# Two layers of attention on one core: which accesses to a PSUM ring are declared independent of each other

## The chip, the cores and the metric

The kernel runs on one core of a Trainium2 chip, in one launch. Its time is the device time of one execution in microseconds (us), and the kernel before is given by the median of three runs. The profile comes from one further execution that was recorded by the hardware profiler.

The engines named here: TensorE (PE in the profile; PEld are its weight loads), VectorE (DVE), ScalarE (ACT), GpSimd (POOL) and SyncE (SP). SP and POOL issue DMAs, each in the order of its own queue.

## The reference

Two images of 256 channels and 64 x 64 pixels pass through two layers; each adds to its input a function of the group-normalised input. Cut to layer 0, which the change concerns:

```python
x = x + _L0_conv_ref(_gn(x), qkv_w, qkv_b, 8)

qkv = jnp.einsum('bchw,oc->bohw', x, qkv_w) + qkv_b[None, :, None, None]
qkv = qkv.reshape(b, 3, num_heads, head_dim, n)          # 8 heads of 32, n = 4096
attn_logits = jnp.einsum('bhci,bhcj->bhij', q, k) * scale
attn_weights = jax.nn.softmax(attn_logits, axis=-1)
out = jnp.einsum('bhij,bhcj->bhci', attn_weights, v)
```

So each head of each image has 4096 x 4096 scores; each row is exponentiated, divided by its sum and multiplied with the values. Group normalisation (32 groups of 8 channels) needs a mean and a variance for each group. Layer 1 is another attention in blocks of 8 x 8 pixels beside a 3 x 3 convolution; the change does not touch it.

## The kernel before

The kernel is written with a framework that finds the dependences between instructions by the tiles they access and inserts semaphore waits. Within layer 0's attention the order on TensorE, ScalarE and VectorE is the order in which the program emits instructions (`manual_schedule`, line 795); SP's and POOL's queues are ordered by the framework.

**Units and groups.** For each image (`b`, two of them) `attention0` runs over 16 groups: 8 heads by 2 halves of the queries. A group has 32 blocks `j` of 128 keys, and each block has 4 units `u` of 512 queries. A unit is a score product of 128 keys by 512 queries (line 522, TensorE), which fills one bank of PSUM, and the exponential of that bank (line 531, ScalarE), which writes a slot in SBUF. There are 28 slots; the profile calls them `es` or `v`, after the two tiles that hold them.

**The ring.** One PSUM tile, `ring`, has 7 banks, used in turn. `scores()` emits one round of 9 units in phases of 1, 1, 3, 2 and 2 (`PHASE`): so many score products, then one exponential over all their banks. A phase is split where it would pass the end of the ring or of the slots. The framework takes a tile as a whole; so in `scores()` each score product is declared independent of the recent exponentials of other banks, and each exponential independent of the recent score products into other banks (`tc.declare_no_dep`).

**What follows the scores.** With a lag of at least 7 units, `work_of` adds a block's exponentials to running sums on VectorE (`add_rows`, lines 572 and 580, into `added`, named `e` in the profile) and multiplies them with the values on TensorE (`quarters`, line 543, four products of 32 columns each, into the accumulator `av`). Seven blocks of a group (`SUMMED`) are not added by VectorE but by accumulating DMAs on POOL's queue (lines 588 and 590), whose result VectorE adds in at the start of the next group (line 770). A slot may be written again when VectorE or the DMA, and TensorE, have read it.

**Spare banks.** Now and then another product needs a bank. `spare_bank()` takes the next bank of the ring out of its turn. Three kinds of use go through the list `wanted`; the main loop takes the bank after a round of scores and runs the use after two further steps of work:

- the sums of rows of the group before (`finish` and `sum_rows`): eight products of `ones` with `added` through `quarters` (line 543, `ring<-e,ones`), then a ScalarE copy out of the bank (line 620, `avs<-ring`). This happens 15 times per image;
- the mean for layer 1's normalisation (`means`, line 318, and the copy of line 319), once per image in the last group;
- the variance (`variances`, line 328, and the copy of line 726), once per image in the last group.

The last group's own sums of rows also use a spare bank, but they are emitted at the end of its scores, with other operands.

**After the sums.** The copied sums go out and back through memory on SP's queue: `dsum` (line 621), `dense` (line 623), the reciprocals on VectorE (lines 626 to 628, at block 9), `drec` (line 629), and back into `avs` (line 631). VectorE multiplies the group's result by them at block 17 (line 635). The same queue brings the next head's keys in four pieces of 512 KB (line 380), its values (line 384), the queries, and in later groups `o` (line 690).

## Time and profile before

| | us |
|---|---|
| median of 3 runs | 3133.02 (3130.93 to 3133.04) |
| the profiled execution | 3135.6 |
| its span, first to last instruction | 3133.7 |
| TensorE busy in the span | 3000.3 (96%) |
| VectorE busy | 2459.8 (78%) |
| ScalarE busy | 2343.5 (75%) |
| the exponentials of line 531 (2596 instructions) | 1985.6 busy |
| the score products of line 522 (4096) | 1081.9 busy |
| the sums of rows over whole banks, line 543 `ring<-e,ones` (240) | 32.8 busy, 49.3 idle before them |

Layer 0's attention of the first image lies from 120 to about 1170 us (with the second half of its projections at the start), of the second image from about 1660 to 2727 us. Between and after them lie layer 1 and the second image's projections, which the change leaves alone. One group of attention takes some 64 us: the sums of rows begin at 199.96, 263.85, 327.48, 391.23 us, and so on.

How to read it: TensorE's matmuls are pipelined, so a matmul's length is longer than the distance to the next one, and "busy" is not "at its peak". A number in brackets behind an instruction is the time its engine sat idle before it, with what ended that time. A wait costs time only where nothing else of equal length runs beside it.

### The profile page before, as it was taken

The page shows a single profiled execution, that of the slowest core. Times are in us where ns is not written, and L with a number is a line of the kernel's source. Part 1 is how long each engine was busy: PE and PEld are TensorE (multiplying, and loading weights), DVE is VectorE, ACT ScalarE, POOL GpSimd, SP SyncE. Part 2 cuts the span into 40 slices and gives each one's busy share as a digit, 9 for nine tenths or more (in the row PEclk, how much of TensorE's full clock was granted, in tenths as well). Part 3 has the DMA queues.
Part 4 walks back from the last instruction along what each step waited for, and adds up shares of the span by engine and source line. Part 5 has one row for each costly group of instructions (what it writes and reads, how often), then busy time and mean ns, then how long its engine had stood idle before and what let it go on. Part 6 is the DMA issues. An engine that isn't in the chain of part 4 may idle for free. (4 is left out here: it accounts for less than half of the span.)

```text
span 3133.7 us, 63967 instructions
## 1 busy us (share of the span) xinstructions
PE 3000.3 (96%) x25129; PEld 1864.8 (60%) x25129; DVE 2459.8 (78%) x3122; ACT 2343.5 (75%) x3262; POOL 836.2 (27%) x923
## 2 busy tenths in 40 slices
PE   6999999999999999999989999999999999899998
PEld 3555555555555556667755555555555555466765
DVE  4599989999899988856556998989988899834543
ACT  2699999999999974632237999999999999734333
POOL 2022222222222221055401222222222222305440
PEclk9999999999999999999999999999999999999999
DMA  7979679786897651231159787796878975600000
GB/s 237 272 136 179 142 152 178 144 176 150 163 180 161 138 126 35 64 125 49 41 186 266 134 169 152 155 181 138 173 161 163 182 152 126 166 4 4 21 14 22
DMA packets 243796, 424.48 MB, mean 135 GB/s; under 512 B 99112, under 2 KB 109916, under 8 KB 241308
## 3 DMA queue, kind: packets, MB, share of 16 engines
q0 software_dynamic: 94992, 238.36, 39.7%
q1 hardware_dynamic: 147580, 181.68, 21.3%
q8 instruction: 199, 3.26, 0.4%
q14 instruction: 113, 0.93, 0.1%
q10 hardware_dynamic: 912, 0.27, 0.0%
HBM read 119.03 MB, written 68.39 MB: 60 GB/s over the span
## 5 line engine op out<-in xcount | busy, mean ns | idle before, releaser
L531 ACT ACTIVATE es<-ring 128x512 f32<-128x512 f32 (+2 forms) x1572 | 1204.3, 905 | 34.8 <-PE ring L522 28.1
L580 DVE TENSOR_TENSOR e<-e,es 128x1024 f32<-128x1024 f32 (+1 forms) x956 | 1039.4, 1145 | 80.8 <-ACT es L531 80.1
L522 PE MATMUL ring<-q,k 128*128 128x512 f32 x4096 | 1081.9, 407 | 4.1 <-ACT es L531 1.9
L522 PEld LDWEIGHTS ring<-q,k 128*128 128x128 f32 x4096 | 733.5, 188 | 373.9 <-ACT es L531 115.6
L531 ACT ACTIVATE v<-ring 128x512 f32<-128x512 f32 (+2 forms) x1024 | 781.3, 902 | 33.7 <-PE ring L522 29.6
L543 PE MATMUL av<-es,v 128*32 128x256 f32 (+1 forms) x9684 | 726.6, 390 | 0.0
L580 DVE TENSOR_TENSOR e<-e,v 128x1024 f32<-128x1024 f32 (+1 forms) x636 | 671.0, 1109 | 49.8 <-ACT v L531 48.3
L543 PE MATMUL av<-v 128*32 128x256 f32 (+1 forms) x6188 | 496.9, 388 | 0.0
L543 PEld LDWEIGHTS av<-es,v 128*32 128x32 f32 x9684 | 328.2, 110 | 267.3 <-issue 108.4
L543 PEld LDWEIGHTS av<-v 128*32 128x32 f32 x6188 | 220.7, 109 | 170.8 <-issue 72.4
L590 POOL DMA_DIRECT2D es<-es x118 | 100.8, 854 | 508.9 <-ACT es L531 463.9
L975 PE MATMUL mm<-v,wf 128*128 128x256 f32 x1024 | 227.6, 380 | 1.5 <-DVE z L984 1.5
L975 PEld LDWEIGHTS mm<-v,wf 128*128 128x128 f32 x1024 | 193.3, 190 | 36.8 <-issue 9.8
L965 POOL TENSOR_TENSOR v<-col 128x512 f32<-128x512 f32 x128 | 165.2, 1316 | 180.1 <-DVE x L996 35.0
L980 ACT COPY z<-mm 128x512 f32<-128x512 f32 x32 | 18.7, 584 | 184.3 <-PE mm L975 184.3
L590 POOL DMA_DIRECT2D acc<-es x118 | 116.5, 987 | 114.2 <-ACT es L531 56.3
L588 POOL DMA_DIRECT2D es<-es x20 | 11.4, 568 | 504.7 <-ACT es L531 401.6
L590 POOL DMA_DIRECT2D es<-v x72 | 61.3, 852 | 316.7 <-ACT v L531 306.1
L981 DVE TENSOR_TENSOR z<-z,mm 128x512 f32<-128x512 f32 x32 | 22.0, 686 | 141.4 <-ACT z L980 141.0
L590 POOL DMA_DIRECT2D v<-es x112 | 114.9, 1026 | 24.3 <-ACT es L531 11.6
L590 POOL DMA_DIRECT2D acc<-v x78 | 77.1, 988 | 69.3 <-DMA acc<-es 23.9
L961 POOL TENSOR_TENSOR col<-xp 128x1152 f32<-128x1152 f32 x32 | 69.3, 2165 | 64.3 <-DVE xp L1394 53.0
(252 smaller groups left out, 2685.3 us busy)
## 6 DMA issues: line engine op xcount, KB each, us to landing
acc<-es POOLq DMA_DIRECT2D x128, 512.0 KB, 6.4
acc<-v POOLq DMA_DIRECT2D x84, 512.0 KB, 6.3
es<-es POOLq DMA_DIRECT2D x138, 256.0 KB, 4.1
v<-es POOLq DMA_DIRECT2D x132, 256.0 KB, 4.9
k<-wk_halves SPq DMA_DIRECT2D x64, 512.0 KB
q<-wq_halves SPq DMA_DIRECT2D x256, 128.0 KB
v<-v POOLq DMA_DIRECT2D x90, 256.0 KB, 5.1
es<-v POOLq DMA_DIRECT2D x84, 256.0 KB, 3.9
```

The costliest lines, as they stand in the source:

```text
L522: made = nc.tensor.matmul(sc[:, i, :], held["k", g // 2][:, j * P : (j + 1) * P], held["q", g, u // 2][:, u % 2, :], start=True, stop=True,)
L531: made = nc.scalar.activation(dst, sc, AF.Exp, scale=SC0)
L543: nc.tensor.matmul(dst[HD0 * u : HD0 * u + HD0, n], lhs, rhs(u)[:, n], start=start, stop=stop)
L580: nc.vector.tensor_add(dst[:, s, :], dst[:, s, :], src)
L588: nc.gpsimd.dma_start(out=dst, in_=src)
L590: nc.gpsimd.dma_start(out=dst, in_=src, accum_op=ALU.add)
L961: (nc.gpsimd.tensor_add if plus else nc.gpsimd.tensor_sub)(col, cols(one), cols(two))
L965: (nc.gpsimd.tensor_add if plus else nc.gpsimd.tensor_sub)(dst, rows(one), rows(two))
L975: nc.tensor.matmul(mm[:, m, r, :], wf[:, k, 4 * r + q, m * P : (m + 1) * P], v[r // 2][:, r % 2, k, :], start=k == 0, stop=k == KC - 1,)
L980: nc.scalar.copy(z[:, 1], mm[:, :, 1, :])
L981: nc.vector.tensor_add(z[:, 0], z[:, 1], mm[:, :, 0, :])
```

## The change

The bookkeeping that declares accesses independent is pulled out of `scores()` into a function `touch`, with one list for all engines, and the users of a spare bank are passed through it too: the first-to-fifteenth groups' sums of rows and their copy, the mean's and the variance's products, and their copies. An access is declared independent of every recent access by another engine to other banks. The list keeps the last 60 accesses, where the two lists before kept 21 each. The last group's own sums of rows are not passed through it. Line numbers shift: the score product moves from 522 to 535, the exponential from 531 to 541, `quarters` from 543 to 550, the copy of the sums from 620 to 627.

```diff
         def means(self, ks, pm, copy):
-            nc.tensor.matmul(pm, group8, self.mv[:, ks, 0], start=True, stop=True)
-            copy(self.mean[:, ks], pm)
+            return nc.tensor.matmul(pm, group8, self.mv[:, ks, 0], start=True, stop=True), copy(self.mean[:, ks], pm)
...
-        recent = {"pe": [], "act": []}
+        recent, spare = [], [0]
         ring = psum["sc"].tile([P, BANKS, T], F32, tag="ring", name=f"ring_{b}")
+
+        def touch(made, banks):
+            for engine, past, other in recent:
+                if engine != made.ins.engine and not banks & other:
+                    tc.declare_no_dep(made.ins, past.ins, reason="another bank of the ring")
+            recent.append((made.ins.engine, made, banks))
+            del recent[:-60]
+            return made
+
+        def touch_spare(made):
+            return touch(made, {spare[0]})
 
         def spare_bank():
...
             n_places += 1
-            return ring[:, (n_places - 1) % BANKS, :]
+            spare[0] = (n_places - 1) % BANKS
+            return ring[:, spare[0], :]
...
-                        made = nc.tensor.matmul(
+                        touch(nc.tensor.matmul(
                             sc[:, i, :], held["k", g // 2][:, j * P : (j + 1) * P], held["q", g, u // 2][:, u % 2, :],
                             start=True, stop=True,
-                        )
-                        for past, taken_of in recent["act"]:
-                            if at % BANKS + i not in taken_of:
-                                tc.declare_no_dep(made.ins, past.ins, reason="another bank")
-                        recent["pe"] = (recent["pe"] + [(made, at % BANKS + i)])[-21:]
+                        ), {at % BANKS + i})
                     ((_, dst),) = at_places(at, m)
-                    made = nc.scalar.activation(dst, sc, AF.Exp, scale=SC0)
-                    for past, of in recent["pe"]:
-                        if of not in banks:
-                            tc.declare_no_dep(made.ins, past.ins, reason="another bank")
-                    recent["act"] = (recent["act"] + [(made, banks)])[-21:]
+                    touch(
+                        nc.scalar.activation(dst, sc, AF.Exp, scale=SC0), set(range(at % BANKS, at % BANKS + m))
+                    )
...
-            quarters(rows, ones, lambda u: added[g][u // 2][:, u % 2, :], True, True)
+            quarters(rows, ones, lambda u: added[g][u // 2][:, u % 2, :], True, True, None, touch_spare)
...
-            nc.scalar.copy(avs[:, 1, :], rows)
+            touch_spare(nc.scalar.copy(avs[:, 1, :], rows))
...
+        def mean_of_first(bank):
+            for made in st.means(first_chunk, bank[:, 0:1], nc.scalar.copy):
+                touch_spare(made)
+
         def variance_of_first(bank):
-            st.variances(first_chunk, bank[:, 0:1])
-            nc.scalar.copy(st.d[:, first_chunk], bank[:, 0:1])
+            touch_spare(st.variances(first_chunk, bank[:, 0:1]))
+            touch_spare(nc.scalar.copy(st.d[:, first_chunk], bank[:, 0:1]))
 
         at_block(last, 5, lambda: st.aggregate(first_chunk))
-        at_block(last, 6, lambda: wanted.append(lambda bank: st.means(first_chunk, bank[:, 0:1], nc.scalar.copy)))
+        at_block(last, 6, lambda: wanted.append(mean_of_first))
```

`quarters` takes a further argument, `note`, through which each of its products is passed.

More of the change, by code (lines that the diff above doesn't have):

```diff
@@ L327, in variances @@
         def variances(self, ks, pv):
-            nc.tensor.matmul(pv, group8, self.d[:, ks], start=True, stop=True)
+            return nc.tensor.matmul(pv, group8, self.d[:, ks], start=True, stop=True)
         def deviations(self, ks, pv):
@@ L516, in scores @@
                 for at, m in list(runs_of(min(size, n_units - len(places)))):
-                    banks = set(range(at % BANKS, at % BANKS + m))
                     sc = ring[:, at % BANKS : at % BANKS + m, :]
@@ L521, in scores, with quarters @@
                         g, (j, u) = unit // (4 * NJ), divmod(unit % (4 * NJ), 4)
-                        made = nc.tensor.matmul(
+                        touch(nc.tensor.matmul(
                             sc[:, i, :], held["k", g // 2][:, j * P : (j + 1) * P], held["q", g, u // 2][:, u % 2, :],
                             start=True, stop=True,
-                        )
-                        for past, taken_of in recent["act"]:
-                            if at % BANKS + i not in taken_of:
-                                tc.declare_no_dep(made.ins, past.ins, reason="another bank")
-                        recent["pe"] = (recent["pe"] + [(made, at % BANKS + i)])[-21:]
-                    ((_, dst),) = at_places(at, m)
-                    made = nc.scalar.activation(dst, sc, AF.Exp, scale=SC0)
-                    for past, of in recent["pe"]:
-                        if of not in banks:
-                            tc.declare_no_dep(made.ins, past.ins, reason="another bank")
-                    recent["act"] = (recent["act"] + [(made, banks)])[-21:]
+                        ), {at % BANKS + i})
+                    ((_, dst),) = at_places(at, m)
+                    touch(
+                        nc.scalar.activation(dst, sc, AF.Exp, scale=SC0), set(range(at % BANKS, at % BANKS + m))
+                    )
                     places.extend(range(at, at + m))
                     n_places = at + m
-        def quarters(dst, lhs, rhs, start, stop, part=None):
+        def quarters(dst, lhs, rhs, start, stop, part=None, note=lambda made: made):
             n = slice(0, T) if part is None else slice(part * T // 2, (part + 1) * T // 2)
             for u in range(4):
-                nc.tensor.matmul(dst[HD0 * u : HD0 * u + HD0, n], lhs, rhs(u)[:, n], start=start, stop=stop)
+                note(nc.tensor.matmul(dst[HD0 * u : HD0 * u + HD0, n], lhs, rhs(u)[:, n], start=start, stop=stop))
         def unit(g, j, u):
```

## The prediction

> **What bounds the kernel now.** I read the page's summary first (TensorE busy 96% of the span of 3133.7 us), then TensorE's waits, because an engine that is nearly always busy can only be helped where it stands still. Columns: engine, what it was about to do, what released it, total us, times, longest us.

> ```profile
> PE ring L543 <- ACT es L531: 24.9, 16, 1.7
> PE ring L543 <- ACT v L531: 22.8, 15, 2.3
> ...
> PE ring L318 <- ACT v L531: 3.3, 2, 1.7
> PE ring L328 <- ACT v L531: 3.1, 2, 1.6
> ```

> Apart from a start-up wait for statistics (L318, 33.8 us), these are the largest waits TensorE has. They are the products into a spare bank: sums of rows (L543 into `ring`) and the two small statistics products (L318, L328). An exponential releases all but one (1.9 us, put down to issue). 30 sums of rows and 4 statistics products stand behind them. The timeline of one such place, TensorE first, then ScalarE (start, length, instruction, idle time before it):

> ```profile
> 261.26 1.07 PE L543 MATMUL av<-v 128*32 128x256 f32 x16
> 263.85 1.07 PE L543 MATMUL ring<-e,ones 128*32 128x512 f32 x8 [1.52 <-ACT es L531]
> 264.73 1.26 PE L543 MATMUL av<-v 128*32 128x256 f32 x19
> ...
> 266.14 2.35 PE L522 MATMUL ring<-q,k 128*128 128x512 f32 x9
> ```

> ```profile
> 259.54 4.26 ACT L531 ACTIVATE es<-ring 128x512 f32<-128x512 f32 x5 [0.56 <-PE ring L522]
> 264.98 0.58 ACT L620 COPY avs<-ring 128x512 f32<-128x512 f32 x1 [1.19 <-PE ring L543]
> 266.68 3.41 ACT L531 ACTIVATE es<-ring 128x512 f32<-128x512 f32 x5 [1.11 <-PE ring L522]
> ```

> TensorE stops 1.52 us until ScalarE has emptied its whole backlog (last exponential ends 263.80). Then ScalarE has nothing: it idles 1.19 us for the sums, copies, and idles 1.11 us for the next score. So each engine drains the other, once per group. Inside a group neither has much slack: nine units cost ScalarE 4.09 us (start to start 0.477 us for one bank, 0.903 for two, 1.328 for three, in phases 1, 1, 3, 2, 2), and a round of scores and quarter products takes about 4.13 us (206.38 to 210.51 in the timeline). The first exponential after the copy follows its score at 0.54 us, so there TensorE sets the time, and what TensorE saves before it moves everything behind it.

> The granted clock shows a second cost. Columns: window, its length, then busy time of PE, PEld, DVE, ACT, POOL, the clock, DMA.

> ```profile
> 848.20:851.60 3.40, 3.22 (x24) 1.19 (x28) 3.40 (x4) 0.72 (x2) 1.91 (x3) 0.51 0.86 146
> ...
> 1121.30:1124.70 3.40, 3.40 (x27) 1.56 (x28) 2.21 (x5) 0.16 (x1) 0.61 (x1) 0.50 1.05 207
> 1138.40:1141.80 3.40, 3.40 (x20) 1.88 (x18) 3.24 (x5) 1.01 (x3) 0.70 (x1) 0.50 1.05 187
> 2694.90:2698.30 3.40, 3.40 (x12) 2.12 (x14) 3.16 (x5) 2.91 (x4) 0.00 (x0) 0.50 1.09 213
> ```

> Four windows of 3.4 us run at half clock inside attention, and each begins during or shortly after one of the 34 waits (848.38, 1121.01, 1137.96, 2692.96). No other wait of attention stands before one.

> **The change, part by part.** *Removed.* A spare-bank product now waits only for the exponential that last read its own bank. That one is 2 to 4 exponentials earlier in ScalarE's order. In the trace it ended 1.88 us or more before each sum of rows began, so TensorE, which waited 1.50 to 2.30 us in idle time, is let through at once or nearly. The sums also need `added`: VectorE's last addition (L770) ended at least 2.29 us before they began, and 3.5 us before the two longest waits. It holds none of them.

> Size: the idle times before the 34 products sum to 55.8 us. Idle time is counted from the end of the product before. Start to start, the 34 pairs take 68.6 us, and quarter products followed by scores that nothing holds start 0.31 us apart, so 34 x 0.31 = 10.5 us would remain. **58.1 us** go. Bounds: 55.8 if a satisfied wait costs another 0.07 us, 61.8 with the 0.20 us that separate two products of equal shape. I take the score row, since a wait instruction stays.

> Does it stay gone behind the product? At 263.85 the sums move to about 262.2, the first score from 266.14 to 264.5, its exponential to 265.0. ScalarE has copied by 264.3 and still idles 0.7 us. Worked in the same way for all 34 places, the idle time left is between 0.3 and 2.3 us, never negative, so the whole saving passes on. What else could hold the exponentials behind it are slots of the 28 units that VectorE or a DMA frees. For slots freed across such a place the smallest slack is 3.3 us for VectorE (2537.3) and 4.8 us for the accumulating DMAs (529.5). The shift is 1.5 to 2.3 us; at 848, 3.9 with the slow window against a slack of 5.5.

> *Half-speed windows.* At 848.38 the copy came 2.00 us after the sums and the next exponential 4.42 us after; at 263.85 it was 1.13 and 2.82: 1.60 us dearer. The mean's product at 1121.01 was followed by an exponential after 3.86 us, its twin at 2677.61 in 2.28: 1.58 us. Four windows: **6.4 us** if they go with the pauses, 0 if not. I take 6.4, as all four follow such a pause.

> [...]

> *Added and moved.* No instruction of work is added, and PE, ScalarE, VectorE and POOL keep their order; 26 more TensorE instructions signal a semaphore, which I price at nothing: 4226 do so already, among products that follow each other at 0.20 us all the same. SP's queue is reordered at three places in each batch. Twice the sums' DMA `dsum` goes ahead of a 512 KB piece of K, and `dense` ahead of the next piece, so one more piece is queued between `dense` and `drec`. Once `dsum` goes ahead of a 512 KB load of `o`. K and `o` have over 10 us of time before use. The sums' way is tighter: `drec` feeds `avs`, which VectorE's L635 waits for in order, with additions queued behind it that free the slots. From SP's and VectorE's timelines:

> ```profile
> 793.50 11.09 SPq L629 DMA_DIRECT2D drec<-dense x1
> ```

> ```profile
> 815.41 0.69 DVE L635 TENSOR_TENSOR avs<-avs 128x512 f32<-128x512 f32 x1 [8.24 <-DMA avs<-drec]
> ```

> Here two pieces of K and V stood between `dense` and `drec`: the issue was held 11.09 us and VectorE 8.24 us. That group took 65.3 us and the next 65.1, where others take 63.7. The second holds the slow window of 848, which explains its excess, so the price is the first's 1.6 us. Four groups get one more piece, two a load of `o`: 0 to 6 x 1.6 = 9.6 us. I take **3 us**, nearer to nothing, as `drec` was held only 0.34 and 0.43 us at 275.98 and 534.49, with V alone between, and one piece is added there.

> **Sum:** 58.1 + 6.4 - 3 = 61.5 us. The profiled execution took 3135.6 us (span 3133.7 and 1.9 around it), so 3074.1 by its own time. The runs' median is 3133.0, 2.6 lower: **3071.5 us**.

> **The rivals.**

> (a) *The slow windows stay*, or come behind other pauses: 58.1 - 3 = 55.1, **3078 us**. For it: windows fall by some clock of their own, and pauses of 1.85 us (199.96) and 2.12 (2405.75) drew none. Against: all four of attention's follow such a pause.

> [...]

> (b) *The sums' way on SP gets late* in all six places: 58.1 + 6.4 - 9.6 = 54.9, **3078 us**. For it: the 11.09 us above. Against: at four of the six one piece is added to V, where two stood at 793.5.

> (c) *The stall only moves.* TensorE passes the sums and stops at the next scores, whose banks ScalarE has not read. The scores come 1.86 to 2.29 us after the sums, so even moved ahead they start after the last old exponential has ended. Against it: the 0.3 to 2.3 us left above. Or the finer declarations leave the real waits as they are: **3133 us**.

> (d) *Slower: one queue decides.* `drec` behind more K is held so long that VectorE's stall exceeds the slots' slack. An 8.24 us stall cost 1.6 us, so some 6.6 us are hidden; beyond that each us counts fully. To eat 64.5 us, six groups must lose 10.8 us each: stalls of 17.4 us, `drec` held about 20 us where it was 11.09. At 24 us each group loses 14 us: 6 x 14 - 64.5 = 20 us slower, **3153 us**. Against: no issue of attention was held longer than 11.09 us.

> (e) *More*: the 0.20 us row and no loss on SP: 61.8 + 6.4 = 68.2, **3065 us**.

> **How the numbers follow.** Forecast 0.62, (a) 0.12, (b) 0.10, (c) 0.05, (d) 0.04, (e) 0.07. Range **3063 to 3087**: from (e) with 2 us of spread among runs to (a) and (b) together (58.1 - 9.6 = 48.5 us saved, 3084.5) and as much spread. About 0.2% or 6 us can be told from no change. Faster 0.92: the forecast, (a), (b), (e) and a hundredth of (c), in which some of the stalls would still go. Same 0.04 from the rest of (c), slower 0.04 from (d).

> **What would show it.** Right: TensorE's waits before `ring` at L543, L318, L328 (new lines 550, 317, 327) fall from 54 us to a few; ScalarE's wait for the copy L620 falls from 36.8 us to near 0; common groups last about 62.0 us instead of 63.7; no clock of 0.5 between 200 and 1160 us; VectorE's wait at L635 near its old 25.8 us. Wrong: the first score after a sum of rows waits for an exponential; exponentials wait for VectorE (L580, L572) by more than the old 1 us; `drec` held over 11 us in several groups.

## The result, and the profile after

| | before | after |
|---|---|---|
| median, us | 3132.82 (4 runs, 3130.93 to 3133.04) | 3077.84 (4 runs, 3076.37 to 3078.72) |
| span of the profiled execution | 3133.7 | 3076.7 |
| TensorE busy | 3000.3 (96%) | 2991.9 (97%) |

The ratio is 0.9825, with a 95% interval of 0.9808 to 0.9842: 55.0 us less, and 57.0 us less by the profiled spans. A second measurement of the same two kernels (e10 below) gives 50.4 us.

TensorE's waits of the kernel after come first (what it was about to do, what released it, total us, times, longest us):

```profile
PE ring L535 <- ACT v L541: 6.2, 3, 3.0
...
PE ring L535 <- ACT es L541: 2.7, 4, 1.7
...
PE ring L550 <- DVE e L587: 0.9, 2, 0.5
```

Of the sums of rows (now L550 into `ring`) two still wait, 0.9 us together, and for VectorE's additions. The statistics products are gone from the list. What stands above them is small but new: score products (L535) that wait for an exponential up to 3.0 us. More of that below.

The same place in a group as before, TensorE and then ScalarE (start, length, instruction, idle time before it):

```profile
258.09 1.07 PE L550 MATMUL av<-v 128*32 128x256 f32 x16
258.98 1.04 PE L550 MATMUL ring<-e,ones 128*32 128x512 f32 x8
259.83 1.25 PE L550 MATMUL av<-v 128*32 128x256 f32 x19
...
261.24 2.37 PE L535 MATMUL ring<-q,k 128*128 128x512 f32 x9
```

```profile
256.36 4.27 ACT L541 ACTIVATE es<-ring 128x512 f32<-128x512 f32 x5 [0.56 <-PE ring L535]
260.47 0.64 ACT L627 COPY avs<-ring 128x512 f32<-128x512 f32 x1
261.84 2.49 ACT L541 ACTIVATE es<-ring 128x512 f32<-128x512 f32 x4 [0.74 <-PE ring L535]
```

The sums begin at 258.98 while ScalarE is still inside its backlog, which ends with the copy at 260.47. They have no bracket any more: TensorE did not stop. ScalarE reaches the copy at once, and then idles 0.74 us for the next score, where it idled 1.19 and 1.11 us before. At all 30 places ScalarE's idle time ahead of the copy is 0, and ahead of the next exponential 0.12 to 0.74 us. Common groups last 61.8 to 62.6 us (63.5 to 64.0 before).

Not every group got shorter by its pause. Those that begin with the sums at 765.1, 2292.3, 895.0 and 2421.3 last 68.1, 67.2, 63.1 and 64.4 us; the same groups before, less their pause, make 63.4, 62.8, 62.1 and 63.0. ScalarE's waits (columns as above) and its timeline in the first of them show why:

```profile
ACT v L541 <- DMA acc<-v: 8.9, 4, 4.1
```

```profile
785.50 0.61 ACT L541 ACTIVATE v<-ring 128x512 f32<-128x512 f32 x1
790.20 4.75 ACT L541 ACTIVATE v<-ring 128x1536 f32<-128x1536 f32 x6 [4.09 <-DMA acc<-v]
```

The exponential at 790.20 had its scores. It waited 4.09 us for the slot it writes, which an accumulating DMA was still reading. In the kernel before, this wait came to 0.3 us over the whole run. TensorE next waits 3.04 us for a bank at 791.70, and the clock drops (window, length, busy of PE, PEld, DVE, ACT, POOL, granted clock, DMA share, GB/s):

```profile
791.00:797.80 6.80, 6.10 (x29) 3.82 (x33) 2.30 (x3) 6.70 (x9) 2.17 (x4) 0.50 1.10 205
2320.20:2323.60 3.40, 3.25 (x17) 1.76 (x20) 1.43 (x3) 3.40 (x7) 1.69 (x2) 0.50 1.06 203
```

The four half-speed windows that the prediction named are gone. These are new, the first of them twice as long, and each comes with a stall of TensorE (3.0 and 2.9 us).

What was moved is seen in SyncE's queue. First the kernel before, then after (start, time that the issue took):

```profile
770.69 0.61 SPq L690 DMA_DIRECT2D o<-ctx  x1
...
784.88 0.51 SPq L621 DMA_DIRECT2D dsum<-avs  x1
785.43 1.23 SPq L380 DMA_DIRECT2D k<-wk_halves  x1
```

```profile
767.42 0.50 SPq L628 DMA_DIRECT2D dsum<-avs  x1
767.97 0.44 SPq L697 DMA_DIRECT2D o<-ctx  x1
768.45 1.02 SPq L379 DMA_DIRECT2D k<-wk_halves  x1
771.30 0.34 SPq L630 DMA_DIRECT2D dense<-dsum  x1
771.68 1.64 SPq L379 DMA_DIRECT2D k<-wk_halves  x2
773.42 0.65 SPq L383 DMA_DIRECT2D v<-vals  x1
779.63 11.41 SPq L636 DMA_DIRECT2D drec<-dense  x1
```

Before, `o` was issued 14 us ahead of `dsum` and had landed when the keys came: from 775 to 785 us the mean DMA share was 0.47. After, `o`, three pieces of K and V (512 KB each) go out within 6.1 us (767.97 to 774.07). An accumulating DMA issued at 775.34 on GpSimd's queue takes 14.7 us to land. The one at the same place of the kernel before (issued at 792.97) took 11.3 us (out and in, engine, number, size, us from issue to landing; after, then before):

```profile
acc<-v POOLq DMA_DIRECT2D x1, 512.0 KB, 14.7
```

```profile
acc<-v POOLq DMA_DIRECT2D x1, 512.0 KB, 11.3
```

The earlier one landed at 804.3, and the exponential that needed its slot began at 804.46. That place had next to no room before the change.

VectorE's wait for the copied-back sums grew too:

```profile
DVE avs L642 <- DMA avs<-drec: 45.3, 11, 7.6
```

It was 25.8 us before. What it costs is a question for the experiments.

### The profile page after: what moved, and what is told of

It is laid out like the page before. It is cut to its first block, busy times and chain, and to the rows that moved or that the text cites. A ratio compares the mean times of both kernels' runs of the same rounds, so it can differ in the third digit from the quotient of the medians.

```text
span 3076.7 us, 63947 instructions
## 1 busy us (share of the span) xinstructions
PE 2991.9 (97%) x25129; PEld 1865.1 (61%) x25129; DVE 2455.0 (80%) x3122; ACT 2339.2 (76%) x3262; POOL 837.5 (27%) x923
## 3 DMA queue, kind: packets, MB, share of 16 engines
q8 instruction: 199, 3.26, 0.4%
## 5 line engine op out<-in xcount | busy, mean ns | idle before, releaser
L535 PE MATMUL ring<-q,k 128*128 128x512 f32 x4096 | 1085.0, 408 | 11.4 <-ACT v L541 6.2
L535 PEld LDWEIGHTS ring<-q,k 128*128 128x128 f32 x4096 | 734.5, 188 | 383.2 <-ACT es L541 114.8
L550 PE MATMUL av<-es,v 128*32 128x256 f32 (+1 forms) x9684 | 725.8, 389 | 0.0
L587 DVE TENSOR_TENSOR e<-e,v 128x1024 f32<-128x1024 f32 (+1 forms) x636 | 669.8, 1109 | 25.2 <-ACT v L541 24.2
L550 PE MATMUL av<-v 128*32 128x256 f32 (+1 forms) x6188 | 498.4, 389 | 0.0
L550 PEld LDWEIGHTS av<-es,v 128*32 128x32 f32 x9684 | 328.1, 110 | 265.9 <-issue 106.4
L550 PEld LDWEIGHTS av<-v 128*32 128x32 f32 x6188 | 221.5, 110 | 170.8 <-issue 72.3
L986 PEld LDWEIGHTS mm<-v,wf 128*128 128x128 f32 x1024 | 193.3, 190 | 36.8 <-issue 9.8
L595 POOL DMA_DIRECT2D es<-es x20 | 11.4, 568 | 505.1 <-ACT es L541 414.8
L597 POOL DMA_DIRECT2D v<-es x112 | 116.7, 1042 | 19.6 <-ACT es L541 10.2
```

Of the source, the lines that this page charges most:

```text
L535: touch(nc.tensor.matmul(sc[:, i, :], held["k", g // 2][:, j * P : (j + 1) * P], held["q", g, u // 2][:, u % 2, :], start=True, stop=True, ...
L550: note(nc.tensor.matmul(dst[HD0 * u : HD0 * u + HD0, n], lhs, rhs(u)[:, n], start=start, stop=stop))
L587: nc.vector.tensor_add(dst[:, s, :], dst[:, s, :], src)
L597: nc.gpsimd.dma_start(out=dst, in_=src, accum_op=ALU.add)
L986: nc.tensor.matmul(mm[:, m, r, :], wf[:, k, 4 * r + q, m * P : (m + 1) * P], v[r // 2][:, r % 2, k, :], start=k == 0, stop=k == KC - 1,)
```

## The experiments

Ten further runs, in three sets. e1 to e4 ran beside 19 runs of the kernel before (median 3132.34), e5 to e7 beside nine (3131.71), e8 to e10 beside nine (3131.28). All edits are to the kernel after; e10 is that kernel itself.

**e1, the sums alone.** The mean's and the variance's products and copies are not declared.

```diff
-            for made in st.means(first_chunk, bank[:, 0:1], nc.scalar.copy):
-                touch_spare(made)
+            st.means(first_chunk, bank[:, 0:1], nc.scalar.copy)
...
-            touch_spare(st.variances(first_chunk, bank[:, 0:1]))
-            touch_spare(nc.scalar.copy(st.d[:, first_chunk], bank[:, 0:1]))
+            st.variances(first_chunk, bank[:, 0:1])
+            nc.scalar.copy(st.d[:, first_chunk], bank[:, 0:1])
```

> The changed kernel with the two statistics products and their copies not declared independent; the sums of rows stay declared. Theory (TensorE's pause before each spare-bank product is the whole cost, 1.82 us each start to start, and the half-speed windows follow the pauses): the 4 statistics pauses come back (4 x 1.82 = 7.3 us) and with them up to 3 half-speed windows of 1.6 us (1121, 1138 and 2694 before): 3078 + 7 to 12 = 3085 to 3090 us; TensorE waits before ring at L318 and L327 of 6 to 7 us, none at L550. Rival (the windows fall by a clock of their own): 3085 us and no window behind these four.

Measured: 3085.45 (3083.15 to 3087.22), ratio 0.9846 [0.9830, 0.9863], 46.9 us less than before. TensorE's waits:

```profile
PE ring L318 <- ACT v L541: 3.4, 2, 1.7
PE ring L327 <- ACT v L541: 3.1, 2, 1.6
```

and the windows behind the second image's two pauses:

```profile
2629.20:2632.60 3.40, 3.40 (x15) 2.27 (x8) 2.84 (x7) 1.34 (x3) 0.00 (x0) 0.51 1.16 200
2646.30:2649.70 3.40, 3.40 (x9) 2.34 (x8) 2.98 (x4) 2.38 (x3) 0.04 (x1) 0.50 1.11 218
```

The four pauses come back with their old length. Both of the second image's drew a window; the same two pauses of the first image drew none. The two stalls of the kernel after are there as well, each with a window (792.9 and 2322.0).

**e2, the statistics alone.** The sums of rows and their copy are not declared.

```diff
-            quarters(rows, ones, lambda u: added[g][u // 2][:, u % 2, :], True, True, None, touch_spare)
+            quarters(rows, ones, lambda u: added[g][u // 2][:, u % 2, :], True, True)
...
-            touch_spare(nc.scalar.copy(avs[:, 1, :], rows))
+            nc.scalar.copy(avs[:, 1, :], rows)
```

> The changed kernel with the 30 sums of rows and their copies not declared independent; the statistics stay declared. Theory: only 4 pauses go (7.3 us) and three windows (4.8 us), so 3133 - 7 to 12 = 3121 to 3126 us, TensorE waits at L550 before ring 49 us as before. Rival (SP's reordered queue costs more than the 11 us that are missing from the forecast): the time would lie well under 3121, since SP's queue then keeps its old order.

Measured: 3124.86 (3119.61 to 3131.18, 10 runs), 0.9975 [0.9964, 0.9985], 7.5 us less.

```profile
PE ring L550 <- ACT es L541: 24.9, 16, 1.7
PE ring L550 <- ACT v L541: 22.5, 14, 2.3
```

The sums' waits are what they were before the change. The two parts add up to 46.9 + 7.5 = 54.4 us, against 55.0 for both by the first measurement and 50.4 by e10's. Behind the 30 pauses that are left, this profiled execution has no half-speed window; the kernel before has one behind these (848.2).

**e3, products but not copies.** The sums and the two statistics products are declared, the ScalarE copies out of their banks are not.

```diff
-            touch_spare(nc.scalar.copy(avs[:, 1, :], rows))
+            nc.scalar.copy(avs[:, 1, :], rows)
...
-            for made in st.means(first_chunk, bank[:, 0:1], nc.scalar.copy):
-                touch_spare(made)
+            touch_spare(st.means(first_chunk, bank[:, 0:1], nc.scalar.copy)[0])
...
-            touch_spare(nc.scalar.copy(st.d[:, first_chunk], bank[:, 0:1]))
+            nc.scalar.copy(st.d[:, first_chunk], bank[:, 0:1])
```

> The changed kernel with the spare-bank products declared independent but the ScalarE copies out of the bank not: the next scores wait for the copy again. Theory: the drain of ScalarE's backlog goes as in the changed kernel, but the scores that follow stand 0.13 us (14 places with 24 quarter products between) or 0.56 us (16 places with 16 between) behind the copy: 14 x 0.13 + 16 x 0.56 = 10.8 us lost, 3089 us. Rival (the copy is never the later one): 3078 us. Rival (both declarations are needed for any gain): 3130 us.

Measured: 3084.95 (3083.19 to 3086.51), 0.9842 [0.9826, 0.9859], 47.4 us less: against the whole change 7.6 us are lost by its first measurement (55.0 us less) and 3.0 by e10's (50.4 us less), fewer than was expected. TensorE's waits hold a new group:

```profile
PE ring L535 <- ACT avs L627: 5.1, 15, 0.5
```

The next round's first score now waits for the copy, though the copy reads another bank. ScalarE's idle time ahead of the next exponential is 0.59 us in a common group.

**e4, copies but not products.**

```diff
-            quarters(rows, ones, lambda u: added[g][u // 2][:, u % 2, :], True, True, None, touch_spare)
+            quarters(rows, ones, lambda u: added[g][u // 2][:, u % 2, :], True, True)
...
-            for made in st.means(first_chunk, bank[:, 0:1], nc.scalar.copy):
-                touch_spare(made)
+            touch_spare(st.means(first_chunk, bank[:, 0:1], nc.scalar.copy)[1])
...
-            touch_spare(st.variances(first_chunk, bank[:, 0:1]))
+            st.variances(first_chunk, bank[:, 0:1])
```

> The changed kernel with only the copies declared independent of the scores in other banks; the products into the spare bank still wait for the whole backlog. Theory: TensorE still stops 1.5 to 2.3 us before each of the 34 products and the scores that follow the copy never waited for it by much: 3130 to 3133 us, TensorE waits at L550 before ring 45 us or more. Rival (the copy's wait was half of the cost): about 3105 us.

Measured: 3132.82 (3128.07 to 3139.83, 10 runs), 0.9998 [0.9988, 1.0008]: nothing.

```profile
PE ring L550 <- ACT es L541: 24.9, 16, 1.7
PE ring L550 <- ACT v L541: 22.8, 14, 2.3
```

Declaring the copies is worth nothing alone, and 3 to 8 us once the products are free. Here windows stood at 199.7, 1121.3, 1138.4, 2681.2 and 2698.3 us, in part behind other pauses than before.

The five that follow ask why four groups were longer than their pause allows; e10 is measured beside the last two. One theory is the prediction's: `drec` is held, VectorE waits for `avs`. The other is the burst: `o`, K and V at once make the accumulating DMAs late.

**e5, `o` later.** `o` is emitted at block 10 instead of 4, which puts it behind `drec`.

```diff
-            in_two((9 + w, 4), (9 + w, 18), add_output(0, w))
+            in_two((9 + w, 4) if w != 1 else (9 + w, 10), (9 + w, 18), add_output(0, w))
```

> The changed kernel with the load of o for two of its blocks (once per image, in the group from 765 us and its twin from 2292) emitted at block 10 instead of block 4: on SP's queue it then stands behind drec instead of between dsum and the pieces of K. Theory (the 512 KB of o, moved by the change from 13 us before the sums into the burst of K, V and the accumulating DMAs, make an accumulating DMA land late, and ScalarE waits 4.1 us for its slot): the waits of line 541 for DMA acc at 790 and 2317 go, both groups return from 68.1 and 67.2 to about 63.4 us, 3078 - 8 to 11 = 3067 to 3070 us. Rival (the groups are simply too short for the DMAs now, whatever SP's order): both groups stay at 67 to 68 us and the time at 3078.

Measured: 3079.48 (3076.60 to 3083.70), 0.9838 [0.9823, 0.9852]. A miss. The longest wait for an accumulating DMA falls to 1.6 us, but `o` now stands between `drec` and `avs`. VectorE, then ScalarE:

```profile
DVE avs L642 <- DMA avs<-drec: 51.6, 12, 10.3
```

```profile
ACT v L541 <- DVE e L587: 4.3, 2, 2.3
```

VectorE's wait of up to 10.3 us is more than the slots' room, and the exponentials wait for VectorE's additions instead (2.0 and 2.3 us). Both groups last 67.6 us, as long as without the edit (68.1 and 67.2). TensorE then stalls for 2.0 and 1.8 us, and a window follows each time (805.8 and 2335.0). So the prediction's way to lose time exists, at a wait of this length.

**e6, `o` earlier.** Emitted at block 0, so ahead of `dsum`.

```diff
-            in_two((9 + w, 4), (9 + w, 18), add_output(0, w))
+            in_two((9 + w, 4) if w != 1 else (9 + w, 0), (9 + w, 18), add_output(0, w))
```

> The changed kernel with the same load emitted at block 0 instead of block 4: on SP's queue it stands ahead of dsum, as before the change, and one piece of K with it. Theory: as for the late load, 3067 to 3070 us, groups at 765 and 2292 at about 63.4 us; if the other pieces of K were what matters, no more than half of that. Rival (group length alone): 3078 us.

Measured: 3071.65 (3069.13 to 3073.83), 0.9812 [0.9798, 0.9826]. ScalarE's waits for accumulating DMAs:

```profile
ACT v L541 <- DMA acc<-v: 1.9, 2, 1.0
```

The groups at 766.4 and 2288.9 last 63.1 and 63.2 us, and no window at half clock is left in attention. VectorE still waits 41.7 us for `avs` (45.3 in the kernel after), so that wait can't have been the larger part of the loss.

**e7, K and V later.** They are fetched at block 20 instead of 4, which puts V behind `drec` and `avs`.

```diff
-                if j == 4 and g % 2 == 0 and g // 2 + 1 < NH0:
+                if j == 20 and g % 2 == 0 and g // 2 + 1 < NH0:
```

> The changed kernel with the next head's K and V fetched at block 20 instead of block 4. In SP's queue V then stands behind drec (in every second group), in the groups at 765 and 2292 behind avs; K hardly moves. Theory (the burst between dense and drec holds drec and the accumulating DMAs): drec is held under 1 us in all groups, VectorE's wait for avs at line 642 falls from 45.3 us to under 15 us, and the waits of line 541 for DMA acc fall; 3066 to 3073 us. Rival (o alone is at fault): VectorE's wait falls, the time stays at 3076 to 3079 us.

Measured: 3078.98 (3075.68 to 3082.82), 0.9837 [0.9822, 0.9851]. VectorE's waits, then ScalarE's:

```profile
DVE avs L642 <- DMA avs<-drec: 12.3, 8, 2.9
```

```profile
ACT v L541 <- DMA acc<-v: 7.5, 6, 3.0
...
ACT es L541 <- DMA acc<-es: 5.1, 5, 1.8
```

The way of the sums is free (`drec` takes 0.34 us throughout), VectorE's wait is down by 33 us, and the time is that of the kernel after. `o` and K still made the accumulating DMAs at 776.8 and 2302.6 take 11.7 and 12.7 us, and there are new waits for later ones (at 555.8, 804.7, 813.2 and 2339.9). The rival's numbers held; that `o` alone is at fault is not shown by that.

**e8, `o` in the group before.** Emitted at block 22 of the previous group; the order of K, V, `dsum`, `dense` and `drec` stays as changed.

```diff
-            in_two((9 + w, 4), (9 + w, 18), add_output(0, w))
+            in_two((9 + w, 4) if w != 1 else (8 + w, 22), (9 + w, 18), add_output(0, w))
```

> The changed kernel with only the load of o in question emitted a whole group earlier (block 22 of the group before), so that on SP's queue it is far from the sums, and K, V, dsum, dense and drec keep the changed kernel's order. Theory (the burst's size decides, and o is its last quarter): ScalarE's waits for DMA acc at 790 and 2317 fall from 4.1 and 3.9 us to about 1 us, the two groups last 63 to 65 us instead of 68.1 and 67.2: 3069 to 3074 us. Rival (the piece of K that the early load took along was what helped there): groups of 66 to 68 us, 3076 to 3079 us.

Measured: 3076.38 (3071.95 to 3076.80), 0.9824 [0.9809, 0.9838], by the medians 4.5 us under the kernel after in the same set (e10); the two intervals overlap, and the median lies above the expected range. In the profiled executions the two groups last 64.0 and 64.1 us (66.0 in e10), and the two waits are down to 1.3 us, both as expected, with `drec` still held 9.8 and 10.4 us. By the time, `o` accounts for a part of the loss only.

**e9, `o`, K and V all earlier.** e6, and K and V fetched at block 0: everything goes ahead of `dsum`.

```diff
-            in_two((9 + w, 4), (9 + w, 18), add_output(0, w))
+            in_two((9 + w, 4) if w != 1 else (9 + w, 0), (9 + w, 18), add_output(0, w))
...
-                if j == 4 and g % 2 == 0 and g // 2 + 1 < NH0:
+                if j == 0 and g % 2 == 0 and g // 2 + 1 < NH0:
```

> The changed kernel with o emitted at block 0 and the next head's K and V at block 0 instead of 4: all four pieces of K and V then stand ahead of dsum on SP's queue. Theory (what stands between dsum and avs makes the sums' way long, and what is loaded at the same time as the accumulating DMAs makes them late): VectorE's wait for avs falls from 45.3 to under 20 us, drec is nowhere held over 3 us; the waits for DMA acc stay or move a little earlier, as the bytes are the same: 3066 to 3072 us. Rival: dsum, now behind K and V, comes late and VectorE waits at line 633 or 642 by more than before: 3075 us or more.

Measured: 3067.67 (3065.44 to 3068.71), **0.9795 [0.9780, 0.9810]**, faster than both kernels: 63.6 us under the one before, 13.2 under e10. SyncE's queue, then ScalarE's waits:

```profile
754.41 0.48 SPq L697 DMA_DIRECT2D o<-ctx  x1
754.94 1.51 SPq L379 DMA_DIRECT2D k<-wk_halves  x3
756.67 0.58 SPq L383 DMA_DIRECT2D v<-vals  x1
767.17 3.29 SPq L628 DMA_DIRECT2D dsum<-avs  x1
773.73 0.34 SPq L630 DMA_DIRECT2D dense<-dsum  x1
779.67 0.34 SPq L636 DMA_DIRECT2D drec<-dense  x1
```

```profile
ACT v L541 <- DMA acc<-v: 0.4, 1, 0.4
ACT es L541 <- DMA acc<-es: 0.3, 1, 0.3
```

The same transfers go out in a tighter train, 13 us earlier. `dsum` is held 3.29 us by them, `drec` no longer. VectorE's wait for `avs` is gone, but its wait for `dense` has grown, as the rival said, without the loss that the rival saw in it (67.2 us here, 42.7 in the kernel after):

```profile
DVE span L633 <- DMA dense<-dsum: 67.2, 18, 6.7
```

The two accumulating DMAs of `v` between 765 and 795 us land in 5.8 us at the median. The burst still slows one, issued just behind it at 758.99:

```profile
acc<-es POOLq DMA_DIRECT2D x1, 512.0 KB, 12.8
```

It lands at 771.84, and the exponential that needs its slot begins at 771.92, after a wait that the profile puts down to its score. So the collision is not gone; it now meets a DMA that just has the time. The groups that began at 765, 2292, 895 and 2421 us now last 63.1, 62.6, 61.9 and 61.9 us.

**e10, the changed kernel again**, unedited, beside e8 and e9.

> The changed kernel itself, beside the two others on the same chip: 3076 to 3080 us.

Measured: 3080.85 (3076.54 to 3082.06), 0.9834 [0.9819, 0.9850]. The two groups last 66.0 us each, with waits for accumulating DMAs of 3.82 and 3.26 us, and a half-speed window behind the second of them at 2323.5. Behind the first, TensorE stalled 2.75 us until 791.84, and the clock stayed up where the kernel after had lost it at the same place:

```profile
791.00:794.40 3.40, 2.38 (x8) 1.27 (x8) 2.77 (x4) 3.40 (x5) 1.37 (x2) 1.00 1.18 210
```

## Why the prediction was right, and where its sum was off

*The pauses* (58.1 us taken, 55.8 to 61.8 as bounds): right in mechanism, slightly small. The quarter products and the sums behind them now follow each other at 0.196 us start to start, the statistics products at 0.309. So 30 x 0.196 + 4 x 0.309 = 7.1 us remain of 68.6, and 61.5 us went. The row of 0.20 us was the right one; a wait instruction that is satisfied costs nothing that the profile shows. Rival (c), that the stall only moves, fell: the first score after the sums waits for no exponential.

*That it stays gone behind the product*: right, with 0.12 to 0.74 us of ScalarE's idle time left at the 30 sums. e3 and e4 add what the prediction had left together: the products carry 47.4 us, the copies 3 to 8, and only behind free products.

*The windows* (6.4 us): all four went, but half-speed time came back behind two new stalls, 10.2 us of it where there had been 13.7. So rival (a) held in its second half, that windows come behind other pauses; they are counted under the queue below. e1 shows the link again, and its limit: of four equal pauses two drew one.

The clock records of the traces show part of what decides. Within each trace all windows begin on one grid of 3.413 us (848.25, 1121.31 and 1138.38 lie 80 and 5 steps apart), and the grid lies elsewhere in the next execution. Take TensorE's idle time in each interval of the grid, over both images' attention (without its first 3.4 us, and without intervals already at half clock) in all twelve traces. Behind all 8 intervals with 1.9 us or more the next one was at half clock; behind those with 1.5 to 1.9 us it was in 13 of 69; behind the 7024 with less, never. So in these traces a stall counted by what of it fell into one interval: the 3.04 us of the kernel after put 2.32 into the one from 787.6, and the next was at half clock; e10's stall of 2.75 us fell into two, which held 1.85 and 1.08 us of idle time, and neither was followed by a window. Outside attention the border is less sharp: in the kernel after, 1.75 us drew no window (the interval from 1251.8), 1.64 us drew one (from 1152.8). The pauses before the change lie at the border, and there idle time alone does not decide: the statistics products' pauses drew a window at 9 of 12 places (kernel before, e1, e4), the sums' at 2 of 90 (kernel before, e2, e4), at much the same length. That the windows depend on the pauses is shown; that the median runs lost just four of them, 6.4 us, is not.

Waits of quite different length had half clock behind them: 0.50 was granted behind a TensorE stall of 3.04 us here, and behind pauses of 1.7 and 1.6 us in e1.

*SP's order* (3 us taken, 0 to 9.6 as bounds): this is the step that failed, in size and in kind. Its price was to be VectorE's wait for `avs`, in units of 1.6 us, read from one group. (In e9 nothing holds `drec` and VectorE does not wait for `avs`, and that group still lasts 1.3 us longer than the next; so the 1.6 us need not have been `drec`'s.) The four groups named above are longer than before less the pause by 4.7, 4.4, 1.0 and 1.4 us, 11.5 in all with the new windows in them: above the upper bound. (Against e9, which also takes away what such a group lost before the change, it is 13.3 us.) VectorE's wait for `avs` did rise, from 25.8 to 45.3 us, and `drec` was held between 5.1 and 11.4 us in six groups of the first image (3.2 to 11.1 in four before). But that wait is nearly all hidden: e6 keeps 41.7 us of it and stands 60.1 us under the kernel before, where the changed kernel stood 55.0 and 50.4 us under it; e7 takes 33 us of it away and gains nothing, though with V moved onto other DMAs. What was paid for was the burst: an accumulating DMA landed late (14.7 us), an exponential lacked its slot (4.09 us), TensorE lacked its bank (3.04 us), the clock dropped (0.50 for 6.8 us). Each of these four steps is in the profile of the group at 765.

The prediction had looked at just that resource and found room of 4.8 us. It looked only at slots freed across a pause, where its shift would bite, and not at the slots in the middle of a group, where the room was about 0.2 us (804.3 landed, 804.46 needed). Nor did its list of signs name a wait for `acc`. Two of the signs for being right failed: VectorE's wait did not stay near 25.8 us, and there was a clock of 0.5 at 791 us.

The terms as measured: 61.5 + 6.4 - 11.5 = 56.4 us, against 57.0 by the spans. The agreement is better than the sum deserves. From the first to the sixteenth sums of each image, where 32 of the 34 pauses lie, the spans fell by 26.2 and 24.2 us, 50.4 in all, where the terms give 32 x 1.81 + 6.4 - 11.5 = 52.8; some 3 us of the 57.0 came from stretches that the change does not touch. (From the first image's sixteenth sums to the second's first, the kernel after and e10, the same program, took 587.3 and 592.0 us.) The two errors, 3.4 us too little for the pauses and 8.5 too little for the queue, partly cancelled; the forecast came out low, by 6.3 us against the medians. Rivals (a) and (b) both name the right total (3078): (b) by the wrong way, (a) with windows that came back but the queue still at 3 us.

*Slower by the queue* (d): not reached, but e5 shows its mechanism at work, from a VectorE wait of about 10 us.

Left open: e8's median lies between those of e10 and e6, and how much of the gain is `o` itself, and how much its distance from K, is not decided. In e9 the train of 2.5 MB is no smaller, only earlier, and it still makes one accumulating DMA take 12.8 us; that this one had the room is read from the trace, and no run varied the moment by steps. Why some intervals with 1.5 to 1.9 us idle draw a window and most do not was not found.

## What to carry to other kernels

When a tile is a ring of buffers, every use of one of its buffers, the rare one too, has to be declared or tracked by the buffer: 34 rare products cost 61.5 us here, 2% of the run. When a stall goes, look in the queue's new order for what now goes out together (here `dsum` went 14.2 us behind `o` before, and 0.55 us ahead of it after), and check the room of everything that waits for a DMA through the whole stage, not only where the stall was. Where a large load is emitted is worth a run of its own: emitting `o`, K and V earlier gave another 13 us here. And a clock term should be read off more than one profiled execution: in attention the kernel after spent 10.2 us at half clock behind its stalls in one and 3.4 us in the other (e10).

## What the runs showed of the hardware that was not expected

An accumulating DMA of 512 KB on GpSimd's queue took 6.1 to 6.4 us to land at the median of both kernels, but 11.3 us (before), 14.7 us (after) and 12.8 us (e9, at 758.99) while SyncE's queue had K, V or `o` under way.

SyncE's issue of an 8 KB `drec` took 0.34 to 2.43 us where V alone went out between `dense` and it (kernel before), 3.19 to 8.65 us with one piece of K and V, and 10.0 to 11.4 us with two pieces and V (both kernels). This is time of SyncE's own instruction: in the kernel after it lasted 11.41 us from 779.63, and the next one in its order, `avs`, began at 794.86. With a piece of K and no V between (e7) it took 0.34 us.
